# Whole blocks stored stripe by stripe, and the column marks summed on GpSimd instead of VectorE

## The chip, the cores and the metric

The kernel runs on one core of a Trainium2 chip. The metric is the device time of one execution in microseconds. Five engines work side by side: TensorE (PE; its weight loads are shown as PEld), VectorE (DVE), ScalarE (ACT), GpSimd (POOL) and SyncE (SP, which here only issues DMAs). Each engine takes its instructions strictly in the order in which they were written.

## The reference

Four graph layers work on x (4096 nodes, 128 features) and one matrix adj (4096 x 4096, float32). Each is preceded by a normalisation and a ReLU, and its result is added to x:

```
h = max(layernorm(x), 0)
0: x += h @ Ws.T + (adj @ h) @ Wn.T + b          1: x += Chebyshev sum: adj @ h, 2 adj @ (adj @ h) - h
2: x += attention over adj.T (exp of leaky relu)  3: x += aggregate of gelu(s_i + d_j + b) * adj[i,j], gelu, layernorm
```

The matrix is sparse, and very unevenly so: entry (i, j) is present with probability about w_i w_j / 1024, w falling as the square root of the index, and the diagonal is full. All values are positive.

## The kernel before, in words

The host reorders the nodes and hands over adj and its transpose adjT. The 4096 rows are 32 blocks of 128 (NB). For the products the columns are cut into 16 stripes of 256 (RS for rows of the result, CS for columns). A stripe is multiplied with some blocks whole ("near" blocks, 112 pairs of stripe and block for the rows) and with the rest of its rows only where something stands in them: these rows are listed, gathered 128 at a time and called a chunk (68 chunks for row stripes, `rseg`, 74 for column stripes, `cseg`). Gathered chunks are stored again in DRAM tables r_tab and c_tab, so that later layers load them without gathering.

**The first stage** reads all of adj (64 tiles of 1 MB, `read_adj`, L766), once. For each block b:

- ACT turns it into an fp8 mask of 128 x 4096 (`mark`, L776), four mask buffers in all.
- DVE clears the diagonal (`scan`, L787), then makes three passes over the mask read as 1024 words of four marks: the largest word of each of the 16 column stripes goes into `col_raw[:, :, b]` (L791, one reduction), the words are joined with their own number (L796), and words without a mark are set to zero (L798). Then eight largest values are picked out of each segment of words (L805, MAX8) into `cand`; from these the positions of all entries are decoded later (`entries`).
- PE counts marks for the row stripes (L704), and `row_flags` and `pairs` (L635 to L683, small DVE operations and a few matmuls) turn this into the list of rows that each row stripe needs. There is one `words` tile.

When the last block is through L791, `all_marked` is set, and `col_flags` (L717, then `pairs`) makes the lists of the column stripes.

**Gathers.** All gathers go through GpSimd (L551): for layer 0 a chunk of adjT (`rseg`) and one of the features (`g`) for each of the 68 row chunks, for layers 1 and 2 the features alone, 74 `cseg` chunks and 74 chunks of attention features, 158 gathers of single entries (`e_val`) and 158 gathers of messages in layer 3 (`m`, `tau`, `e`): 736 in all. The `cseg` gathers need the column lists, so they can only begin when all 32 blocks are marked; `e_val` needs the decoded entries. Beside this GpSimd adds a bias to x (L987, four instructions of 1024 values per partition; L1008, eight of 512).

**Loads of near blocks and of tables** (`Layer.load`, L1092 and L1104; `Attention.batches`, L1206) are issued by SP into four `big` tiles. A near tile of up to four blocks is 128 partitions by up to four pieces of 256 floats; in adj and adjT each piece of 1 KB lies 16 KB from the next row's. The table stores are L730.

**Order.** A planner on the host simulates the engines with rough durations (a gather counts 1.27 us) and writes the instructions in the order of its simulated times; every generator above yields the engine, a duration and, by the rank with which it was started, a priority (lower goes first among those that could start at the same time). On the chip the order of each engine is then fixed, whatever the real times are.

Of the kernel before, what the change touches and what calls it, by code (L numbers as in the profile page):

```python
# [12 lines left out]
F32 = mybir.dt.float32  # L13
# [12 lines left out]
N = 4096  # L26
D = 128
P = 128
# [329 lines left out]
def on_dve(n):  # L358
    return "DVE", 0.16 + 1.05e-3 * n
# [16 lines left out]
GATHER = "POOL", 1.27  # L376


def sparse_stack(tc, x, adj, adjT, diag, w_self, w_neigh, b0, w1, b1, w2, att_src, att_dst,
                 msg_s, msg_d, msg_b, upd_h, upd_a, upd_b, ln_w, ln_b, out):  # L380


# [7 lines left out]
    with ExitStack() as ctx:  # L390
# [34 lines left out]
        u_tab = table("u_tab", N + 1, D)  # L425
        a_tab = table("a_tab", N + 1, D + 2)
        d_tab = table("d_tab", N, D)
        r_tab = [table(f"r_tab{s.index}", s.cap * P, RS) if s.cap else None for s in ROWS]
        c_tab = [table(f"c_tab{s.index}", s.cap * P, CS) if s.cap else None for s in COLS]

        def rows_in(tab):
            return tab[0:N, :].rearrange("(b p) d -> p b d", p=P)
# [280 lines left out]
        def col_flags(s):  # L713
            yield all_marked
            lane = yield lanes
            yield on_dve(NB)
            nc.vector.tensor_scalar(lane["f"], col_raw[:, s.index, :], EMPTY, None, op0=ALU.is_gt)  # L717
            yield from pairs(s, lane, fetch_col, seg_col, CS, col_list[s.index])

        row_list = [Event() for _ in ROWS]  # L720
        col_list = [Event() for _ in COLS]
        r_done = [Count(s.cap) for s in ROWS]
        c_done = [Count(s.cap) for s in COLS]
        all_marked = Event()

        def store(ready, t, slots, left, dst, done, size):

# [11 lines left out]
        def fetch_columns():  # L739
            for s in COLS:  # L740
                if s.cap:
                    yield col_list[s.index]
                for k in range(s.cap):
                    t = yield csegs
                    yield GATHER
                    gather(t, adj_segments, seg_col[:, s.chunk + k:s.chunk + k + 1])
                    here, left = Event(), Count(1)
                    here.set(plan.transfer(P * CS * 4))
                    plan.start(store(here, t, csegs, left, c_tab[s.index][k * P:(k + 1) * P, :], c_done[s.index],
                                     P * CS * 4), 6)  # L750
                    plan.start(give_back(left, csegs, t), 0)

# [17 lines left out]
        def mark():  # L770
            for b in range(NB):
# [6 lines left out]
                    plan.release(raws, raw_of[b, h])  # L778
                marked[b].set(plan.finish)

        def scan():
            for b in range(NB):
                yield marked[b]
                mask = mask_of[b]
                yield on_dve(32)
                own = mask.bitcast(I32)[:, b * P // 4:(b + 1) * P // 4]
                nc.vector.tensor_tensor(own, own, off_diag.bitcast(I32), op=ALU.bitwise_and)  # L787
                bare[b].set(plan.finish)
                plan.start(give_back(mask_left[b], masks, mask), 0)
                yield on_dve(WORDS)  # L790
                nc.vector.tensor_reduce(col_raw[:, :, b], mask.bitcast(F32).rearrange("p (s w) -> p s w", w=CS // 4),  # L791
                                        axis=AX.X, op=ALU.max)
                if b == NB - 1:
                    all_marked.set(plan.finish)
                yield on_dve(WORDS)
                nc.vector.tensor_tensor(words, mask.bitcast(I32), spread, op=ALU.bitwise_or)  # L796
                yield on_dve(WORDS + 250)
                nc.vector.scalar_tensor_tensor(words.bitcast(F32), mask.bitcast(F32), EMPTY, words.bitcast(F32),  # L798
                                               op0=ALU.is_gt, op1=ALU.mult)
                mask_left[b].set(plan.finish)  # L800
                for u in UNITS:
                    if u.block == b:
                        yield "DVE", 0.15 * len(u.segments) + (u.cuts[-1] - u.cuts[0]) / 960
                        for k, (lo, hi) in enumerate(u.segments):
                            nc.vector.max(cand_of[u.number][:, 8 * k:8 * k + 8], words.bitcast(F32)[:, lo:hi])  # L805
                        picked[u.number].set(plan.finish)

        picked = [Event() for _ in UNITS]
        valued = [Count(u.cap) for u in UNITS]
# [263 lines left out]
        class Layer:  # L1073
# [12 lines left out]
            def load(self):  # L1086
                for s in ROWS:
                    for i, blocks in enumerate(s.tiles(TOGETHER)):
                        t = yield bigs
                        yield SP  # L1090
                        n = len(blocks)
                        nc.sync.dma_start(  # L1092
                            as_rows(t)[:, :n, :], adjT[blocks[0] * P:(blocks[-1] + 1) * P, s.lo:s.lo + RS].rearrange(
                                "(b p) i -> p b i", p=P))
                        self.at["near", s.index, i] = t
                        self.near_here[s.index][i].set(plan.transfer(n * P * RS * 4))
                    if self.number == 0 or not s.cap:
                        continue
                    yield r_done[s.index]
                    for i, chunks in enumerate(s.groups(TOGETHER)):  # L1100
                        t = yield bigs
                        yield SP
                        n = len(chunks)
                        nc.sync.dma_start(  # L1104
                            as_rows(t)[:, :n, :], r_tab[s.index][chunks[0] * P:(chunks[-1] + 1) * P, :].rearrange(
                                "(c p) i -> p c i", p=P))
                        self.at["list", s.index, i] = t
                        self.list_here[s.index][i].set(plan.transfer(n * P * RS * 4))

            def gather(self):  # L1110
                for s in ROWS:
                    if s.cap:
                        yield row_list[s.index]
                    for c in range(s.cap):
                        if self.number == 0:
                            t = yield rsegs
                            yield GATHER
                            gather(t, adjT_segments, seg_row[:, s.chunk + c:s.chunk + c + 1])
                            here, left = Event(), Count(2)
                            here.set(plan.transfer(P * RS * 4))  # L1120
                            self.at["seg", s.index, c] = t, here, left
                            plan.start(store(here, t, rsegs, left, r_tab[s.index][c * P:(c + 1) * P, :],
                                             r_done[s.index], P * RS * 4), 2)
                            plan.start(give_back(left, rsegs, t), 0)
                        g = yield rows_g
                        yield self.table_done
                        yield GATHER
                        gather(g[:, :D], self.table, fetch_row[:, s.chunk + c:s.chunk + c + 1])
                        self.at["row", s.index, c] = g
                        self.rows_here[s.index][c].set(plan.transfer(P * D * 4))  # L1130
# [51 lines left out]
        class Attention:  # L1182
# [11 lines left out]
            def batches(self):  # L1194
                for number, (s, blocks, chunks) in enumerate(self.units()):
                    t = yield bigs
                    here = Event()
                    if chunks:
                        yield c_done[s.index]
                    n = len(blocks or chunks)  # L1200
                    yield SP
                    if blocks:
                        src = adj[blocks[0] * P:(blocks[-1] + 1) * P, s.lo:s.lo + CS]
                    else:
                        src = c_tab[s.index][chunks[0] * P:(chunks[-1] + 1) * P, :]
                    nc.sync.dma_start(t[:, :n, :], src.rearrange("(k p) i -> p k i", p=P))  # L1206
                    here.set(plan.transfer(n * P * CS * 4))
                    rows = []
                    for c in chunks or ():
                        g = yield rows_g  # L1210
                        rows.append((g, Event()))
                    if chunks:
                        plan.start(self.rows(s, chunks, rows), 0)
                    plan.start(self.attend(s, t, here, blocks, chunks, rows), number * 1e-3)
# [352 lines left out]
        with tc.tile_pool(name="scan", bufs=1) as scanning:  # L1567
# [1 line left out]
            masks = tiles(scanning, "mask", 4, (P, N), F8)  # L1569
            raws = tiles(scanning, "raw", 1, (P, HALF))  # L1570
            raws = Slots([dst[:, :HALF], dst[:, HALF:]] + raws.items)
            words = scanning.tile([P, WORDS], I32, name="words", tag="words")
            plan.filler = fill
            plan.start(read_x(), -9)
            plan.start(read_adj(), -8)
# [96 lines left out]
def gnn_stack_kernel(tc, **args):  # L1672


    some_bad = sparse_stack(tc, **args)
    with tc.If(some_bad > 0):
        args.pop("diag")
        dense_stack(tc, **args)


# [293 lines left out]
            nc.sync.dma_start(out_rows[:, s, :], o)  # L1974


# [31 lines left out]
```

## Time and profile before

| What | Value |
|---|---|
| timed runs, median of 3 | 1175.17 us (1168.04 to 1184.51) |
| profiled execution, first to last instruction | 1172.0 us |
| PE busy | 965.2 us (82%) |
| DVE busy | 887.9 us (76%) |
| POOL busy | 771.8 us (66%), 831 instructions |
| ACT busy | 577.5 us (49%) |
| DMA | 236.04 MB, mean 201 GB/s |

No separate time of the profiled execution is on hand; its span lies inside the range of the timed runs, 3.2 us under their median. "Busy" is the time in instructions; the profile puts register, semaphore and DMA-issuing instructions outside it, so an engine with a fixed pause between its instructions can be fully used at less than 100%. PE's share holds 732 filler matmuls (L617) that the planner puts into its gaps, and is no measure of a bound.

### The profile page before, as it was taken

How to read it: one execution, taken by the hardware profiler on the slowest of the kernel's cores; microseconds unless marked ns; L12 is line 12 of the kernel's file. 1: busy time of each engine (PE TensorE's matmuls, PEld its weight loads, DVE VectorE, ACT ScalarE, POOL GpSimd, SP SyncE). 2: the span in 40 equal slices, each digit the busy share in tenths (PEclk: the TensorE clock that was granted, in tenths of full speed). 3: DMA queues.
4: the chain of work that ended last, by engine and by line, in shares of the span. 5: the costliest groups of instructions: out<-in, count | busy, mean ns of one | idle time of the engine just before them, and what ended most of it. 6: DMA issues, size and time to landing. Idle time of an engine off the chain costs nothing. (4 is left out here: it accounts for less than half of the span.)

```text
span 1172.0 us, 19272 instructions
## 1 busy us (share of the span) xinstructions
PE 965.2 (82%) x5782; PEld 669.7 (57%) x5782; DVE 887.9 (76%) x3443; ACT 577.5 (49%) x1228; POOL 771.8 (66%) x831
## 2 busy tenths in 40 slices
PE   5888887878888888788888879899999976678783
PEld 2555665545555665576676654455555555566562
DVE  5799988877878886576888866665666585577895
ACT  3985556654622212232434457576767652234553
POOL 5127746545437677777777778777777777777770
PEclk9979989888789999998989989898999878889997
DMA  7999999999846978889865653443445222222321
GB/s 221 348 349 394 349 407 359 352 309 334 294 127 174 301 217 275 245 272 315 247 204 175 184 150 97 127 129 102 131 131 154 71 69 67 54 68 68 77 74 33
DMA packets 175417, 236.04 MB, mean 201 GB/s; under 512 B 22452, under 2 KB 155336, under 8 KB 167112
## 3 DMA queue, kind: packets, MB, share of 16 engines
q1 hardware_dynamic: 148904, 186.45, 46.9%
q0 software_dynamic: 26400, 48.27, 16.7%
q8 instruction: 48, 0.79, 0.3%
q14 instruction: 65, 0.53, 0.1%
HBM read 203.41 MB, written 31.23 MB: 200 GB/s over the span
## 5 line engine op out<-in xcount | busy, mean ns | idle before, releaser
L551 POOL DMA_INDIRECT e_val<-in_adj,e_at x158 | 163.0, 1032 | 48.0 <-issue 40.1
L551 POOL DMA_INDIRECT g<-h_tab,fetch_row x136 | 134.6, 990 | 41.1 <-issue 27.9
L551 POOL DMA_INDIRECT rseg<-in_adjT,seg_row x68 | 68.8, 1012 | 90.3 <-issue 42.3
L1146 PE MATMUL acc<-big,hA 128*128 128x256 f32 x448 | 122.0, 415 | 2.0 <-DMA big<-in_adjT 2.0
L617 PEld LDWEIGHTS <-nothing 128*128 128x128 f16 x732 | 74.9, 105 | 82.0 <-issue 20.7
L617 PE MATMUL pick<-nothing 128*128 128x512 f16 x430 | 114.2, 413 | 0.0
L551 POOL DMA_INDIRECT cseg<-in_adj,seg_col x74 | 70.9, 958 | 43.6 <-issue 17.3
L1146 PEld LDWEIGHTS acc<-big,hA 128*128 128x128 f32 x448 | 89.4, 210 | 14.5 <-DMA big<-in_adjT 2.6
L776 ACT ACTIVATE mask<-dst 128x2048 fp8e4<-128x2048 f32 x43 | 81.8, 1904 | 26.8 <-DMA dst<-in_adj 26.7
L551 POOL DMA_INDIRECT m<-d_tab,e_col x79 | 76.8, 972 | 24.1 <-issue 13.4
L551 POOL DMA_INDIRECT g<-a_tab,fetch_col x74 | 75.7, 1023 | 22.5 <-issue 12.5
L1163 PE MATMUL acc<-big,g 128*128 128x256 f32 x272 | 77.4, 417 | 9.7 <-DMA big<-r_tab 6.5
L1243 DVE TENSOR_TENSOR tau<-e,big 128x512 f32<-128x512 f32 (+3 forms) x61 | 54.5, 893 | 38.2 <-ACT e L1239 34.0
L551 POOL DMA_INDIRECT tau<-d_tab,e_col x67 | 66.2, 988 | 21.2 <-issue 11.3
L617 PE MATMUL bank<-nothing 128*128 128x512 f16 x302 | 79.8, 401 | 0.0
L551 POOL DMA_INDIRECT g<-u_tab,fetch_row x68 | 64.5, 949 | 20.7 <-issue 8.8
L577 ACT ACTIVATE junk<-xN,stat 128x128 f32<-128x128 f32 x128 | 51.3, 401 | 49.0 <-DVE stat L573 38.5
L1146 PE MATMUL acc<-big,hB 128*128 128x256 f32 x224 | 60.9, 411 | 11.3 <-DMA big<-in_adjT 11.3
L1163 PE MATMUL acc<-rseg,g 128*128 128x256 f32 x136 | 53.4, 501 | 16.8 <-DMA g<-h_tab,fetch_row 16.7
L898 DVE SCALAR_TENSOR_TENSOR ehit<-ehit,pos,pick 128x32 f32<-128x32 f32 (+7 forms) x158 | 38.7, 285 | 36.2 <-ACT ehit L895 35.9
L1163 PEld LDWEIGHTS acc<-big,g 128*128 128x128 f32 x272 | 52.6, 207 | 21.4 <-issue 7.5
L895 ACT COPY ehit<-pick 128x192 f32<-128x192 f32 (+7 forms) x74 | 20.4, 287 | 89.3 <-PE pick L892 78.1
(322 smaller groups left out, 2553.1 us busy)
## 6 DMA issues: line engine op xcount, KB each, us to landing
dst<-in_adj SPq DMA_DIRECT2D x43, 1024.0 KB
big<-in_adjT SPq DMA_DIRECT2D x45, 512.0 KB
raw<-in_adj SPq DMA_DIRECT2D x21, 1024.0 KB
big<-in_adjT SPq DMA_DIRECT2D x66, 256.0 KB
big<-r_tab SPq DMA_DIRECT2D x30, 512.0 KB
c_tab<-cseg SPq DMA_DIRECT2D x74, 128.0 KB
r_tab<-rseg SPq DMA_DIRECT2D x68, 128.0 KB
big<-c_tab SPq DMA_DIRECT2D x15, 512.0 KB
```

Source lines behind the costliest of these rows:

```text
L551: nc.gpsimd.indirect_dma_start(out=dst, out_offset=None, in_=table[:, :], in_offset=bass.IndirectOffsetOnAxis(ap=index, axis=0))
L577: nc.scalar.activation(junk, src[:, k, :], AF.Square, bias=st[:, 0, k:k + 1], accum_out=st[:, 1, k:k + 1])
L617: nc.tensor.matmul(idle[2][idle[1]], nothing[:, :P], nothing, start=True, stop=True)
L776: nc.scalar.activation(mask[:, h * HALF:(h + 1) * HALF], raw_of[b, h], AF.Sigmoid, scale=1e38, accum_out=marks[:, 2 * b + h:2 * b + h + 1] ...
L895: nc.scalar.copy(hit, pv[:, :, :W])
L898: nc.vector.scalar_tensor_tensor(hit[:, q, :], hit[:, q, :], pos0[:, k + q:k + q + 1], pv[:, q, W:2 * W], op0=ALU.is_le, op1=ALU.mult, acc ...
L1146: nc.tensor.matmul(acc, self.near[:, b, :D], as_rows(t)[:, k, :], start=count == 0, stop=count == every - 1)
L1163: nc.tensor.matmul(acc, row[:, :D], r, start=count == 0, stop=count == every - 1)
L1243: nc.vector.tensor_mul(tau[:, :n, :], e[:, :n, :], a[:, :n, :])
```

## The change

Two things are changed.

The layout: the host passes two further copies of the matrix, `adj_near` and `adjT_near`, in which each stripe's blocks lie one beside the other for each of the 128 partitions, and r_tab and c_tab are laid out in the same way. A near tile or a table tile of four blocks is then one run of 4 KB per partition instead of four runs of 1 KB. Numbers and sizes of the DMAs stay. The gathers still read adj and adjT.

The marks: the reduction L791 leaves DVE. In its place a new task adds up, on GpSimd, the words that L798 leaves (zero where nothing stands, positive otherwise) for each stripe: six additions that halve 64 words to 32, 16, 8, 4, 2 and 1. So `words` has two tiles, given back when both GpSimd and MAX8 are through with them, and `all_marked` counts the sums of all 32 blocks.

```diff
+        def marks_of_columns(b, words, left):
+            sums = words.bitcast(F32).rearrange("p (s w) -> p s w", w=CS // 4)
+            n = CS // 8
+            yield "POOL", 3.1
+            while n:
+                into = halved[:, :, :n] if n > 1 else col_raw[:, :, b:b + 1]
+                nc.gpsimd.tensor_add(into, sums[:, :, :n], sums[:, :, n:2 * n])
+                sums, n = halved, n // 2
+            left.set(plan.finish)
+            all_marked.set(plan.finish)
...
-                yield on_dve(WORDS)
-                nc.vector.tensor_reduce(col_raw[:, :, b], mask.bitcast(F32).rearrange("p (s w) -> p s w", w=CS // 4),
-                                        axis=AX.X, op=ALU.max)
-                if b == NB - 1:
-                    all_marked.set(plan.finish)
+                words = yield words_of
                 yield on_dve(WORDS)
                 nc.vector.tensor_tensor(words, mask.bitcast(I32), spread, op=ALU.bitwise_or)
...
                 mask_left[b].set(plan.finish)
+                left = Count(2)
+                plan.start(marks_of_columns(b, words, left), -4)
+                plan.start(give_back(left, words_of, words), 0)
...
-            words = scanning.tile([P, WORDS], I32, name="words", tag="words")
+            words_of = tiles(scanning, "words", 2, (P, WORDS), I32)
+            halved = scanning.tile([P, len(COLS), CS // 8], F32, name="halved", tag="halved")
...
-                            as_rows(t)[:, :n, :], adjT[blocks[0] * P:(blocks[-1] + 1) * P, s.lo:s.lo + RS].rearrange(
-                                "(b p) i -> p b i", p=P))
+                            as_rows(t)[:, :n, :], adjT_near[s.index * P:(s.index + 1) * P, blocks[0] * RS:(
+                                blocks[-1] + 1) * RS].rearrange("p (b i) -> p b i", i=RS))
...
-        r_tab = [table(f"r_tab{s.index}", s.cap * P, RS) if s.cap else None for s in ROWS]
+        r_tab = [table(f"r_tab{s.index}", P, s.cap * RS) if s.cap else None for s in ROWS]
...
+def by_stripe(a, size):
+    return a.reshape(NB, P, N // size, size).transpose(2, 1, 0, 3).reshape(N // size * P, NB * size)
```

The loads of r_tab, c_tab and adj_near and the stores into the tables are changed in the same way, and `col_flags` compares `col_raw` with 0.0 instead of the word of four empty marks.

More of the change, by code (lines that the diff above doesn't have):

```diff
@@ L376, with sparse_stack @@
 GATHER = "POOL", 1.27
-def sparse_stack(tc, x, adj, adjT, diag, w_self, w_neigh, b0, w1, b1, w2, att_src, att_dst,
+def sparse_stack(tc, x, adj, adjT, adj_near, adjT_near, diag, w_self, w_neigh, b0, w1, b1, w2, att_src, att_dst,
                  msg_s, msg_d, msg_b, upd_h, upd_a, upd_b, ln_w, ln_b, out):
@@ L427, in sparse_stack @@
         d_tab = table("d_tab", N, D)
-        r_tab = [table(f"r_tab{s.index}", s.cap * P, RS) if s.cap else None for s in ROWS]
-        c_tab = [table(f"c_tab{s.index}", s.cap * P, CS) if s.cap else None for s in COLS]
+        r_tab = [table(f"r_tab{s.index}", P, s.cap * RS) if s.cap else None for s in ROWS]
+        c_tab = [table(f"c_tab{s.index}", P, s.cap * CS) if s.cap else None for s in COLS]
         def rows_in(tab):
@@ L716, in col_flags @@
             yield on_dve(NB)
-            nc.vector.tensor_scalar(lane["f"], col_raw[:, s.index, :], EMPTY, None, op0=ALU.is_gt)
+            nc.vector.tensor_scalar(lane["f"], col_raw[:, s.index, :], 0.0, None, op0=ALU.is_gt)
             yield from pairs(s, lane, fetch_col, seg_col, CS, col_list[s.index])
@@ L723, in sparse_stack @@
         c_done = [Count(s.cap) for s in COLS]
-        all_marked = Event()
+        all_marked = Count(NB)
         def store(ready, t, slots, left, dst, done, size):
@@ L748, in fetch_columns @@
                     here.set(plan.transfer(P * CS * 4))
-                    plan.start(store(here, t, csegs, left, c_tab[s.index][k * P:(k + 1) * P, :], c_done[s.index],
+                    plan.start(store(here, t, csegs, left, c_tab[s.index][:, k * CS:(k + 1) * CS], c_done[s.index],
                                      P * CS * 4), 6)
@@ L806, in scan @@
                         picked[u.number].set(plan.finish)
+                left.set(plan.finish)
         picked = [Event() for _ in UNITS]
@@ L1104, in load @@
                         nc.sync.dma_start(
-                            as_rows(t)[:, :n, :], r_tab[s.index][chunks[0] * P:(chunks[-1] + 1) * P, :].rearrange(
-                                "(c p) i -> p c i", p=P))
+                            as_rows(t)[:, :n, :], r_tab[s.index][:, chunks[0] * RS:(
+                                chunks[-1] + 1) * RS].rearrange("p (c i) -> p c i", i=RS))
                         self.at["list", s.index, i] = t
@@ L1121, in gather @@
                             self.at["seg", s.index, c] = t, here, left
-                            plan.start(store(here, t, rsegs, left, r_tab[s.index][c * P:(c + 1) * P, :],
+                            plan.start(store(here, t, rsegs, left, r_tab[s.index][:, c * RS:(c + 1) * RS],
                                              r_done[s.index], P * RS * 4), 2)
@@ L1202, in batches @@
                     if blocks:
-                        src = adj[blocks[0] * P:(blocks[-1] + 1) * P, s.lo:s.lo + CS]
+                        src = adj_near[s.index * P:(s.index + 1) * P, blocks[0] * CS:(blocks[-1] + 1) * CS]
                     else:
-                        src = c_tab[s.index][chunks[0] * P:(chunks[-1] + 1) * P, :]
-                    nc.sync.dma_start(t[:, :n, :], src.rearrange("(k p) i -> p k i", p=P))
+                        src = c_tab[s.index][:, chunks[0] * CS:(chunks[-1] + 1) * CS]
+                    nc.sync.dma_start(t[:, :n, :], src.rearrange("p (k i) -> p k i", i=CS))
                     here.set(plan.transfer(n * P * CS * 4))
@@ L1676, in gnn_stack_kernel @@
     with tc.If(some_bad > 0):
-        args.pop("diag")
+        for name in ("diag", "adj_near", "adjT_near"):
+            args.pop(name)
         dense_stack(tc, **args)
@@ L1985 @@
     given = {
-        "x": np.asarray(x)[ORDER], "adj": adj, "adjT": adj.T, "diag": np.diagonal(adj).reshape(NB, P).T,
+        "x": np.asarray(x)[ORDER], "adj": adj, "adjT": adj.T,
+        "adj_near": by_stripe(adj, CS), "adjT_near": by_stripe(adj.T, RS), "diag": np.diagonal(adj).reshape(NB, P).T,
         "w_self": np.asarray(L0_gnn_W)[:, :D].T, "w_neigh": np.asarray(L0_gnn_W)[:, D:].T, "b0": L0_gnn_b,
```

## The prediction

> **What bounds the kernel now.** I read the busy shares in 40 slices first (a slice is 29.3 us).
>
> ```profile
> DVE  5799988877878886576888866665666585577895
> ...
> POOL 5127746545437677777777778777777777777770
> ...
> DMA  7999999999846978889865653443445222222321
> ```
>
> There are two stages. Up to slice 11 (some 320 us) DMA stands at 9 and DVE at 7 to 9, while POOL has room. From slice 12 on POOL stands at 7, one slice at 6 and one at 8, to the end. The busy time of each engine in chosen stretches says what the 7 means; the columns are the stretch, its length, then PE, PEld, DVE, ACT, POOL (each with its instructions), clock, DMA share, GB/s.
>
> ```profile
> 348.00:1141.00 793.00, 670.16 (x3606) 474.45 (x3606) 578.76 (x2439) 361.22 (x843) 601.45 (x610) 0.93 0.54 155
> ...
> 60.00:240.00 180.00, 151.82 (x1251) 104.54 (x1249) 163.71 (x494) 113.78 (x173) 101.30 (x94) 0.88 1.01 368
> 87.00:348.00 261.00, 218.18 (x1706) 146.61 (x1704) 222.88 (x702) 143.97 (x221) 139.73 (x135) 0.86 0.92 329
> ```
>
> POOL's instructions in order of time show the pause between two gathers, and the holes of the first stage:
>
> ```profile
> 290.16 1.45 POOL L551 DMA_INDIRECT g<-h_tab,fetch_row  x1 [0.30 <-issue]
> 295.01 1.27 POOL L1008 TENSOR_TENSOR xN<-xN,b_sb 128x512 f32<-128x512 f32 x1 [3.40 <-ACT hB L585]
> 302.59 1.19 POOL L551 DMA_INDIRECT rseg<-in_adjT,seg_row  x1 [6.31 <-PE acc L1163]
> 304.08 0.94 POOL L551 DMA_INDIRECT g<-h_tab,fetch_row  x1 [0.30 <-issue]
> ...
> 348.03 0.96 POOL L551 DMA_INDIRECT cseg<-in_adj,seg_col  x1 [14.61 <-DVE pf L641]
> ```
>
> Each gather is followed by 0.30 us that nothing else can use. From 348 to 1141 us POOL is busy 601.45 us in 610 instructions; with 610 x 0.30 = 183 that is 784 of 793 us, so 9 us are free. **POOL bounds everything after 348 us**, one gather per 1.25 us, and what delays it by a microsecond delays the end by one. The chain that ended last agrees: it runs from the last gathers (1140 to 1145 us) through the last normalisation. Before 348 us POOL has slack: from its first gather at 87 us it is busy 139.73 us in 135 instructions, with pauses 180 of 261 us, which leaves **81 us free**. The listed holes split them: 22 us up to 209 us, 45 from there to 332, 14 in the last wait, for the first column list. How the change spends these 81 us is the whole question.
>
> **The marks on POOL.** The rows that come nearest to the new additions, and the DVE reduction that goes:
>
> ```profile
> L791 DVE TENSOR_REDUCE col_raw<-mask 128x16 f32<-128x1024 f32 x32 | 39.1, 1221 | 2.1 <-ACT mask L776 0.4
> L1008 POOL TENSOR_TENSOR xN<-xN,b_sb 128x512 f32<-128x512 f32 x8 | 10.5, 1310 | 10.4 <-issue 6.9 <-ACT hB L585 3.4
> ```
>
> An undisturbed L1008 takes 1.27 us for 512 values per partition, an undisturbed L987 2.36 us for 1024: 0.18 us plus 2.13 ns per value. The six additions of a block take 16 x (32+16+8+4+2+1) = 1008 values, so 1008 x 2.13 ns + 6 x 0.18 = **3.23 us**. Below: the fixed part vanishes when they follow each other, 2.15 us. Above: the additions wait for DVE. L987 at 67.74 us took 3.18 instead of 2.36 us beside L798; two such waits in a block give 4.9 us. I take 3.7, the sum from the rows and half a wait, nearer to the undisturbed rows, which are most.
>
> Six blocks were reduced before 87 us, when POOL had nothing to gather; those are free. The other 26 cost 26 x 3.7 = 96 us (56 to 127). Stage by stage: up to 209 us there are 13 blocks, 48 us into 22 free, 26 left over; from 209 to 332 another 13, 48 into 45, 29 left over; the last hole takes 14 of overdue gathers of layer 0, so **15 us** run past 348. That is with every hole used. They are not all usable: POOL stands in them for buffers that PE must free (six of 6.3 us), or for ACT before L1008 (3.4 us), with the gathers queued behind, and a sum that waits for L798 now stands in the same queue. I lose a quarter of the 67 us ahead of 332, **17 us** (bounds: none, half). Sum: +32 us.
>
> **What waits for the sums.** The first column list needs the sum of block 31. L791 of that block ended at 326.7 us; L798 ends at 331.5, and with 3.7 us the mark is there at 335.2, while the list's first operation (L717) stood at 332.8: +2 us, inside the hole where overdue gathers run. With them gone it would be 2 us at the end. Behind the sum on POOL stand `rseg` and `g`, for which PE's layer 0 waits. On DVE, L796 of block b+2 waits for the sum of block b; behind it stand `pairs` and with it the next row list. At 9.4 us a block this wait costs nothing unless POOL is two blocks late.
>
> **DVE.** The reduction takes 1.14 us of DVE per block from start to start, 36 us in all. What comes in is a lock, seen in DVE's and POOL's instructions:
>
> ```profile
> 72.71 2.35 POOL L987 TENSOR_TENSOR xN<-xN,b_sb 128x1024 f32<-128x1024 f32 x1 [1.79 <-DVE pair_total L649]
> ```
> ```profile
> 72.76 2.32 DVE L651 SCALAR_TENSOR_TENSOR pst<-pst 128x1 f32<-128x1 f32 x1
> ```
>
> L651 is one value wide and otherwise takes 0.16 us; here it ends when POOL's addition ends. I summed the excess of DVE's instructions during the twelve L987 and L1008: 12.4 us in 20.7 us of additions, 60%. Where MAX8 was running (39.14 us), there was none. Sums of 3.23 us would cost DVE 1.9 us a block at 60%, and less since MAX8 (1.4 us) runs first: 0 to 1.9, I take 1.1. So DVE's saving of 1.14 is given back, net 0, between -36 and +25 us over the stage; DVE is busy 163.71 of 180 us there, so a loss would lengthen the scan. The first row list comes up to 6 us sooner by the early reductions, minus the stalls: 3 us, which the +2 above cancels.
>
> The Trainium skill's page SBUF — State Buffer, section "Who interferes with whom", says that a reduction never contends with GpSimd, while a DVE instruction with two SBUF inputs and a GpSimd one that reads SBUF exclude each other for the whole instruction. That speaks against the change: a pass that doesn't contend is replaced by six that do. The rows agree on the lock, but not on every microsecond: blocked all the time, DVE would lose 3.23 x 32 = 103 us for 36 saved, by the 60% measured at most 62.
>
> **The layout.** By 330 us 17, 22, 2 and 2 near tiles of 512, 256, 384 and 128 KB were loaded, 15.7 MB. At full DMA share the mixed 1 KB and 512 B traffic of 450 to 500 us moved 251/0.84 = 299 GB/s, and the best 10 us of the first stage, mostly 8 KB rows of adj, 413 at 1.06, so 390: 52 against 40 us, so 0 to 12 us of DMA time. I expect half of it on the DMA engines and none at the end: POOL, not DMA, then sets the first stage. After 348 us DMA is at 0.54, and the free 9 us on POOL bound the gain. The stores, the number of DMAs and SP's queue stay as they are.
>
> **Sum.** 1172.0 + 32 + 2 - 3 + 0 = 1203; the median lies 3.2 us above the profiled span, so **1206 us**.
>
> **Rivals.**
> - *The holes hide the sums* (not slower). At 3.23 us a block 20 us are left over at 209 us, 13 x 3.23 = 42 fit into 45, and the last hole takes 14 of the 17: +3, with holes fully used; at 2.15 nothing is left over, and the first list 6 us sooner gives -6. For it: the holes come twice in 18.8 us, just where two blocks are scanned. Against it: up to 163 us POOL has almost no hole. It decides below 3.3 us a block and no hole lost: 1169 to 1187.
> - *The locks feed each other.* DVE blocked by six additions, additions by L796 and L798 (1.22 us each), gathers behind both, row lists later. At 4.9 us a block: 127 + 17 - 81 = 63, and DVE's +25 in part: +55 to +85, 1230 to 1260.
> - *The scan gets faster*, over 2%: DVE gains 36 us, DMA 12. The gathers cannot: POOL's 180 us and 26 x 2.15 us end no sooner than 87 - 6 + 236 = 317, and only if the scan is also 31 us sooner is the end at 1144.
> - *Nothing changes in the packets* (runs still cut to 1 KB): worth nothing at the end here.
>
> **How the numbers follow.** The POOL overflow (+15 to +55, 1190 to 1230) has 0.56, the hidden sums 0.22, the lock loop 0.16, the fast scan 0.06. 2% is 23.5 us, about what these runs, 1.4% apart, can tell from no change: above 1198.7 lie four fifths of the overflow (0.45) and the lock loop, 0.61; faster 0.06; within, 0.33. The range, 1169 to 1250, leaves out the fast scan and the upper half of the lock loop.
>
> **What would show it.** Right: POOL at 7 or more in slices 3 to 11; about 3.7 us of additions per block; no or short holes; the first `cseg` past 355 us or layer 0's gathers past 375; then 1.25 us per gather to the end. Near packets grow and DMA's share falls. DVE's small operations of 0.16 us take 0.5 to 1.2 beside the sums. Wrong: the first `cseg` at or before 348 us with layer 0 done, additions near 2 us, or the order of gathers so altered that POOL idles after 348.

## The result, and the profile after

The changed kernel takes **1215.21 us** (median of four runs, 1213.93 to 1215.5) against 1173.94 us for the kernel before (four runs, 1168.04 to 1184.51): a ratio of **1.0326, interval 1.029 to 1.0363**, so it is slower. The profiled execution of after has a span of 1213.5 us, 41.5 us more than the 1172.0 us of before. In three of the sessions further down every kernel, the one before too, ran about 27% longer (1512.96, 1486.64 and 1485.22 us for before), at a granted clock of 0.80 to 0.84 in place of 0.90 to 0.93; they are called long sessions.

The busy shares of after in 40 slices (a slice is 30.3 us; they are counted from 0, as in the prediction):

```profile
DVE  6798867586677887674868797657667586477896
...
POOL 5568888887877677777777777777777776777770
...
DMA  7998888889875887888876563344445422222221
```

POOL stands at 7 or 8 from slice 3 to slice 12, with one 6 to come; before, it had 3 to 7 in slices 3 to 11. DMA has gone from 9 to 8 in slices 3 to 8, and DVE falls to 5 and 6 at times where it had 7 and 8. The stretches shown of before read so in after (stretch, length, then PE, PEld, DVE, ACT, POOL with their instructions, clock, DMA share, GB/s):

```profile
348.00:1141.00 793.00, 674.88 (x3580) 468.15 (x3581) 568.58 (x2430) 352.90 (x811) 597.81 (x614) 0.92 0.55 158
...
60.00:240.00 180.00, 135.60 (x1024) 89.05 (x1025) 135.62 (x399) 94.38 (x143) 143.00 (x172) 0.79 0.88 309
87.00:348.00 261.00, 201.30 (x1509) 131.19 (x1507) 191.70 (x553) 128.48 (x195) 213.57 (x258) 0.82 0.88 302
```

From 87 to 348 us POOL is busy 213.57 us where it was busy 139.73. Every other engine does less in the same time than before: DVE 191.70 for 222.88, DMA 302 GB/s for 329. The whole stage has become slower, and POOL is the one engine that does more in it. In order of time POOL now looks like this, early in the stage and at its end (start, duration, instruction, and in brackets the idle time before it):

```profile
92.98 0.95 POOL L551 DMA_INDIRECT rseg<-in_adjT,seg_row  x1 [0.31 <-issue]
93.95 1.26 POOL L788 TENSOR_TENSOR halved<-words 128x512 f32<-128x512 f32 x1
95.30 1.99 POOL L788 TENSOR_TENSOR halved<-halved 128x256 f32<-128x256 f32 x4
97.37 0.22 POOL L788 TENSOR_TENSOR col_raw<-halved 128x16 f32<-128x16 f32 x1
97.73 0.96 POOL L551 DMA_INDIRECT g<-h_tab,fetch_row  x1
...
388.73 0.95 POOL L551 DMA_INDIRECT g<-h_tab,fetch_row  x1 [0.30 <-issue]
389.98 0.95 POOL L551 DMA_INDIRECT cseg<-in_adj,seg_col  x1 [0.30 <-DVE sel L632]
```

The holes of 6.3 us and the last one of 14.61 us are gone. The last gather of layer 0 starts at 388.7 us (before 364.3), and the first `cseg` goes out at 390.0 (before 348.0), with nothing but the fixed 0.30 us ahead of it. The costs by group (count, then total busy us, mean ns, then idle time before them):

```profile
L788 POOL TENSOR_TENSOR halved<-halved 128x256 f32<-128x256 f32 (+3 forms) x128 | 67.9, 531 | 10.0
...
L788 POOL TENSOR_TENSOR halved<-words 128x512 f32<-128x512 f32 x32 | 41.7, 1303 | 34.4 <-DVE words L806 29.6 <-DVE pf L709 4.4
...
L788 POOL TENSOR_TENSOR col_raw<-halved 128x16 f32<-128x16 f32 x32 | 10.2, 320 | 2.5
```

(41.7 + 67.9 + 10.2) / 32 = 3.74 us of busy time per block.

### The profile page after: what moved, and what is told of

Read it like the earlier page. It is cut to its first block, busy times and chain, and to the rows that moved or that the text cites. A ratio compares the mean times of both kernels' runs of the same rounds, so it can differ in the third digit from the quotient of the medians.

```text
span 1213.5 us, 19481 instructions
## 1 busy us (share of the span) xinstructions
PE 984.3 (81%) x5798; PEld 673.7 (56%) x5798; DVE 884.7 (73%) x3411; ACT 576.5 (48%) x1228; POOL 893.0 (74%) x1023
## 2 busy tenths in 40 slices
DMA packets 122171, 236.05 MB, mean 195 GB/s; under 512 B 22452, under 2 KB 75592, under 8 KB 113864
## 4 chain that ended last, share of the span: by engine, by line
DVE 29%; PE 22%; DMA 21%; POOL 12%; issue 9%; ACT 4%; SPq 1%; DVEq 0%; POOLq 0%; ACTq 0%
DMA g<-h_tab,fetch_row 5%; POOL e_val L551 5%; PE acc L1158 3%; DMA g<-a_tab,fetch_col 3%; DMA m<-d_tab,e_col 2%; PE acc L1272 2%; PE acc L1274 2%; PE bank L604 2%; POOL g L551 2%; DMA cseg<-in_adj,seg_col 2%; DMA tau<-d_tab,e_col 2%; DMA raw<-in_adj 2%; POOL halved L788 2%; PE bank L617 2%; PE pick L617 2%
## 5 line engine op out<-in xcount | busy, mean ns | idle before, releaser
L617 PEld LDWEIGHTS <-nothing 128*128 128x128 f16 x748 | 79.5, 108 | 89.2 <-issue 28.7
L1158 PE MATMUL acc<-big,hA 128*128 128x256 f32 x448 | 126.1, 424 | 0.9 <-DMA big<-in_adjT_near 0.9
L617 PE MATMUL pick<-nothing 128*128 128x512 f16 x421 | 117.0, 432 | 0.0
L551 POOL DMA_INDIRECT m<-d_tab,e_col x79 | 77.8, 985 | 24.1 <-issue 13.1
L1175 PE MATMUL acc<-rseg,g 128*128 128x256 f32 x136 | 51.5, 476 | 53.5 <-DMA g<-h_tab,fetch_row 53.3
L617 PE MATMUL bank<-nothing 128*128 128x512 f16 x327 | 88.5, 409 | 0.0
L776 ACT ACTIVATE mask<-dst 128x2048 fp8e4<-128x2048 f32 x43 | 81.8, 1903 | 12.7 <-DMA dst<-in_adj 12.6
L551 POOL DMA_INDIRECT tau<-d_tab,e_col x67 | 65.4, 976 | 25.7 <-issue 13.1
L788 POOL TENSOR_TENSOR halved<-halved 128x256 f32<-128x256 f32 (+3 forms) x128 | 67.9, 531 | 10.0
L788 POOL TENSOR_TENSOR halved<-words 128x512 f32<-128x512 f32 x32 | 41.7, 1303 | 34.4 <-DVE words L806 29.6
L630 ACT ACTIVATE sel_t<-iota_row,mids 128x512 f32<-128x512 f32 (+3 forms) x43 | 27.1, 643 | 79.1 <-DVE mids L625 75.8
```

Source lines behind the costliest of these rows:

```text
L551: nc.gpsimd.indirect_dma_start(out=dst, out_offset=None, in_=table[:, :], in_offset=bass.IndirectOffsetOnAxis(ap=index, axis=0))
L617: nc.tensor.matmul(idle[2][idle[1]], nothing[:, :P], nothing, start=True, stop=True)
L630: nc.scalar.activation(lane["t"][:, :n * P], iota_row[:, :n * P], AF.Abs, bias=mids[:, g:g + 1])
L776: nc.scalar.activation(mask[:, h * HALF:(h + 1) * HALF], raw_of[b, h], AF.Sigmoid, scale=1e38, accum_out=marks[:, 2 * b + h:2 * b + h + 1] ...
L788: nc.gpsimd.tensor_add(into, sums[:, :, :n], sums[:, :, n:2 * n])
L1158: nc.tensor.matmul(acc, self.near[:, b, :D], as_rows(t)[:, k, :], start=count == 0, stop=count == every - 1)
```

## The experiments

Theory A: GpSimd's time ahead of the gathers is what costs. Theory B: the strife of GpSimd and VectorE over the words. Theory C: the planner's new order. Theory D: the layout. Theory E stands in the texts of its runs. Each ratio is to the kernel before in the same session.

In a long session GpSimd does not set the end: in the second run with memsets it is busy 463.8 us from 348 to 1141 us, in 482 instructions; with 0.30 us for each that is 608 of 793 us, and 185 are free. So the times of those runs say little of the change. Three of the kernels also have a run outside the long sessions.

### The layout alone

The marks stay on VectorE, with one tile of words:

```diff
-                words = yield words_of
+                yield on_dve(WORDS)
+                nc.vector.tensor_reduce(col_raw[:, :, b], mask.bitcast(F32).rearrange(...), axis=AX.X, op=ALU.max)
...
-                plan.start(marks_of_columns(b, words, left), -4)
```

> The layout alone; the marks stay a reduction on VectorE. Theory A (GpSimd's time): no additions on GpSimd, so its 81 us of free time before 348 us stay free and the end moves by what the scan gains: 1166 to 1176 us, the first cseg gather at 338 to 350 us. Theory B (the lock on VectorE) and theory C (the new order and the later list) expect the same. Rival D (the rows of 32 KB pitch or the two further copies slow the DMAs, whose rate fell from 344 to 302 GB/s in the changed kernel): 1185 us or more and a DMA rate of the first stage near 300 GB/s.

> The layout alone a second time, because the chips of the first calls ran every kernel, the one before too, at some 1500 us, with stage two no longer bound by GpSimd. If the kernel before is near 1174 us beside it: theories A, B and C 1166 to 1178 us and a first cseg at 338 to 352 us; rival D (the layout slows the loads) 1185 us or more. If it is near 1500 again: the same ratio as before, 0.988 to 0.998.

The first: 1509.39 us against 1512.96, ratio 0.9932 (0.988 to 0.9983). The second: **1170.09 us against 1176.44, ratio 0.9971 (0.9941 to 1.0)**. POOL's busy share in the second one's 40 slices:

```profile
POOL 5127746445446777777777777777777777777770
```

Its `cseg` gathers (count; durations in ns as min, median and max; first and last start in us):

```profile
L551 POOL DMA_INDIRECT cseg<-in_adj,seg_col x74: 942/946/1151, 338.9 to 579.1; - x74
```

POOL has its holes again (4 to 6 in slices 5 to 11), and the column lists come 9 us sooner than before. The layout doesn't cost anything; it may be worth up to 0.6%. Theory D falls: over the stretch from 87 to 348 us this kernel moves 329 GB/s, like before (after 302; the 344 in the first text is not the figure of this stretch). The loss comes in with the marks.

### Seven memsets in place of the six additions

VectorE reduces again, and the changed kernel's order, tiles and waits are kept. GpSimd is held for the same time, but touches nothing of VectorE's:

```diff
-            while n:
-                into = halved[:, :, :n] if n > 1 else col_raw[:, :, b:b + 1]
-                nc.gpsimd.tensor_add(into, sums[:, :, :n], sums[:, :, n:2 * n])
-                sums, n = halved, n // 2
+            for _ in range(7):
+                nc.gpsimd.memset(idle, 0.0)
...
+                nc.vector.tensor_reduce(col_raw[:, :, b], mask.bitcast(F32).rearrange(...), axis=AX.X, op=ALU.max)
                 words = yield words_of
```

> As the run without additions, but GpSimd writes seven times 512 zeros per partition for each block (0.48 to 0.54 us each in the profile of before, some 3.5 us a block): its time is taken, and nothing is read. Theory A: the loss is there without the additions' two inputs, 1200 to 1218 us, GpSimd without holes. Theory B (VectorE is held up by the additions' lock): 1168 to 1182 us.

> The new layout, the order of the changed kernel and its waits are kept; the column marks are taken by VectorE's reduction again, and in place of each block's six additions GpSimd runs seven memsets of 128x512, 533 ns each in the earlier run of this kernel, so 3.73 us per block against 3.74 us for the additions. The memsets read nothing that VectorE writes. Theory A (what costs is GpSimd's time in front of the gathers, 26 blocks x 3.7 us): 1195 to 1220 us where the kernel before takes about 1175, first read of a column segment past 375 us. Theory B (what costs is the strife of the two engines over the words): the loss goes with the additions, 1165 to 1182 us, first read of a column segment before 355 us. If the kernel before takes about 1490 us on this chip, A is seen in the first read alone and the time stays within 2%.

> The seven memsets per block once more (VectorE's reduction for the marks, the changed kernel's order and waits, 7 x 533 ns = 3.73 us of GpSimd per block that touch nothing of VectorE's). Where the kernel before takes about 1175 us on this chip: theory A (GpSimd's time in front of the gathers) says 1195 to 1220 us and a first read of a column segment past 370 us; theory B (the strife over the words) says 1165 to 1182 us and a first read before 355 us. Where the kernel before takes about 1490 us: within 2% by both.

In the long sessions: 1470.37 us, 0.9802 (0.9709 to 0.9896), and 1468.85 us, 0.9937 (0.9888 to 0.9986). In the third: **1203.45 us against 1173.1, ratio 1.0268 (1.0223 to 1.0312)**. POOL's slices in its profile:

```profile
POOL 6558888888887677777777777877777776777770
```

The group of its memsets, and then its `cseg` gathers:

```profile
L785 POOL MEMSET idle<- 128x512 f32 x224 | 119.5, 534 | 11.2
```
```profile
L551 POOL DMA_INDIRECT cseg<-in_adj,seg_col x74: 942/946/1192, 380.9 to 620.6; - x74
```

POOL is as full as in after. 119.5 / 32 = 3.73 us per block, with nothing to quarrel over, give 30.35 of the 41.27 us. Theory A is shown for the greater part. The other 10.9 us are open: the strife may have a part in them, but the two intervals just overlap, and this kernel also keeps the reduction on VectorE. As it has the changed order too, theory C is not told apart from A by this run alone; but with the memsets POOL is idle beyond its short pauses for only 8.8 us up to 440 us (below), so something else can hardly have been what it waited for.

### The sums for a part of the blocks

From block 6 or 19 on VectorE reduces, and GpSimd has nothing to add:

```diff
+                if b >= ON_POOL:
+                    yield on_dve(WORDS)
+                    nc.vector.tensor_reduce(col_raw[:, :, b], mask.bitcast(F32).rearrange(...), axis=AX.X, op=ALU.max)
+                    all_marked.set(plan.finish)
                 words = yield words_of
...
-                left = Count(2)
-                plan.start(marks_of_columns(b, words, left), -4)
+                left = Count(1 + (b < ON_POOL))
+                if b < ON_POOL:
+                    plan.start(marks_of_columns(b, words, left), -4)
```

> New layout; only the first 6 blocks are summed on GpSimd, before it has anything to gather, the other 26 reduced on VectorE. Theory A: the sums cost nothing, the first row list comes up to 6 us sooner: 1162 to 1174 us. Theory B: 6/32 of the loss, some +8 against the layout alone. Theory C: like A.

> New layout; the first 19 of the 32 blocks summed on GpSimd, the other 13 reduced on VectorE. Theory A: 13 blocks x 3.7 = 48 us of sums after the first gather against 81 us free, so most of it is hidden: 1170 to 1188 us, and GpSimd has holes again after 209 us. Theory B: in proportion, 19/32 of 41 us: about 1198 us. Theory C (the list waits for the last sum): as with no sums, 1175 us, since the last marks are VectorE's.

> The changed kernel with GpSimd's sums for blocks 0 to 18 alone, and VectorE's reduction for 19 to 31. GpSimd is given 13 blocks x 3.74 = 49 us after its first gather, in place of 97. Theory A (GpSimd's time, with the holes of this stage used whole): 49 us fit into the 81 us that were free, so most is hidden, 1168 to 1188 us. Theory E (every microsecond put in front of the gathers costs the same share, 41.5/97): 13/26 of the loss, 1188 to 1200 us. If the kernel before takes about 1490 us on this chip, neither is told by the time.

> GpSimd's sums for blocks 0 to 18 alone once more, VectorE's reduction for 19 to 31: 13 blocks x 3.74 = 49 us of GpSimd after its first gather in place of 97. Where the kernel before takes about 1175 us on this chip: theory A (the 81 us in which GpSimd had nothing to do in this stage take the sums up first, and only what is over delays the gathers) says 1168 to 1188 us, first read of a column segment by 362 us; theory E (every microsecond put in front of the gathers delays them by the same share, 41.5 of 97) says 1188 to 1200 us, first read at 366 us or later. Where the kernel before takes about 1490 us: within 2% by both.

Long sessions: six blocks 1510.93 us, 0.9977 (0.9948 to 1.0007); nineteen 1494.88, 0.9912 (0.9864 to 0.996), and 1477.37, 0.9934 (0.9888 to 0.9981). Nineteen blocks in the third: **1192.45 us against 1175.4, ratio 1.0123 (1.0085 to 1.0161)**. That is under 2%, with an interval clear of 1, and the time lies in theory E's range, not A's. It also goes against theory C as this kernel's first text has it: the list can't have waited for the last sum, which ended at 235 us. The first read of a column segment, at 363.0 us, lies between the two (by 362, or 366 and later). POOL's slices:

```profile
POOL 5568888864546677777777777877777776777770
```

POOL in order of time after its last sum, which ended at 235 us, and then the `cseg` gathers:

```profile
301.17 0.94 POOL L551 DMA_INDIRECT g<-h_tab,fetch_row  x1 [0.30 <-issue]
307.61 0.94 POOL L551 DMA_INDIRECT rseg<-in_adjT,seg_row  x1 [5.50 <-issue]
...
331.47 0.94 POOL L551 DMA_INDIRECT g<-h_tab,fetch_row  x1 [0.30 <-issue]
339.89 0.94 POOL L551 DMA_INDIRECT rseg<-in_adjT,seg_row  x1 [7.49 <-PE pick L617]
```
```profile
L551 POOL DMA_INDIRECT cseg<-in_adj,seg_col x74: 940/946/1172, 363.0 to 603.8; - x74
```

The holes are back in slices 8 to 12 (4 to 6), and yet the column lists are 15 us late. Free time late in the stage did not make up for what was lost early: what is late by then is the scan. This is followed below.

### The marks alone, the additions left away, the additions twice

The marks alone: before's layout with after's marks. Without additions: the memset kernel above with no memset. Twice: the six additions are run once into `halved` alone and then again:

```diff
+            for into_marks in (False, True):
+                part, n = sums, CS // 8
+                while n:
+                    into = halved[:, :, :n] if n > 1 or not into_marks else col_raw[:, :, b:b + 1]
+                    nc.gpsimd.tensor_add(into, part[:, :, :n], part[:, :, n:2 * n])
+                    part, n = halved, n // 2
```

> The marks alone on GpSimd, the blocks laid out as before. Theories A, B and C: all of the loss, 1208 to 1225 us, first cseg near 390 us, GpSimd without holes from 88 us on, DMA rate near 300 GB/s although the rows are 1 KB again. Rival D: 1175 to 1190 us.

> The changed kernel in its own order of instructions, the planner still counting 3.1 us of GpSimd for each block, but no addition is issued; the reduction stands on VectorE again, at a place that the planner gives no time. Theory A: GpSimd is free again: 1165 to 1182 us, first cseg 335 to 355 us. Theory C (the order that the planner made): it keeps most of the loss, 1200 us or more.

> The changed kernel, its order kept, with the six additions of each block made twice (the first time into a scratch tile). Theory A: GpSimd has no hole left after 88 us, so another 26 x 3.3 to 3.9 us go straight into the time: 1300 to 1320 us. Theory B: VectorE loses another 1 to 1.9 us a block: 1245 to 1275 us. Theory C: no change, 1215 us.

All three fell in long sessions. The marks alone: 1494.17 us, 0.9889 (0.9849 to 0.9928); without additions: 1485.82, 0.9974 (0.9924 to 1.0024); twice: **1579.13, 1.0622 (1.0527 to 1.0717)**. The first `cseg` of the marks alone, then of twice:

```profile
L551 POOL DMA_INDIRECT cseg<-in_adj,seg_col x74: 940/946/1144, 395.2 to 712.1; - x74
```
```profile
L551 POOL DMA_INDIRECT cseg<-in_adj,seg_col x74: 940/946/1155, 502.5 to 815.0; - x74
```

A second set of sums moves the first read by 107 us, about the 27 x 3.74 = 101 us that such a set takes after the first gather (the two kernels differ in layout and session too). So even where the end has another bound, the first stage follows GpSimd's time once it is full. In the other kernels of these sessions the first read came between 381 and 403 us, with sums and without (384.3 for the layout alone, 338.9 in the session where the kernel before took 1176), so their ratios below 1 say nothing for the change where the kernel before takes 1174.

Theory C can be set against these traces. In after, with the memsets, without additions and with the additions twice, the work of GpSimd, VectorE and ScalarE and the DMAs of SyncE come in one and the same order, marks left aside. Yet the first read is at 390.0 us in after and at 502.5 in twice, though twice fell in a long session; with the memsets it comes at 381 us in long and other sessions alike. And in one session, at the same order, SP waits between 60 and 390 us for late chunks (L730) 7.2 us without additions and 83.8 us with the memsets. So GpSimd's time, and not the order alone, moves the first stage. That the order costs nothing is not shown: the kernel without additions has the latest of those other first reads, 403.0 us, although its chunks were not late, and it was run in a long session only.

## Why the prediction was right

The forecast was 1206 us, slower, range 1169 to 1250; 1215.21 was measured. POOL's time from its first gather up to 440 us, when all five kernels were long gathering without holes, shows the balance. All values are in us and summed from the trace's instructions; of each idle time the first 0.31 us count as pause, the rest as hole.

| Kernel | Length | Gathers: number, busy | Sums or memsets | Bias | Pauses | Holes |
|---|---|---|---|---|---|---|
| before | 352.8 | 197, 196.0 | 0 | 10.5 | 60.3 | 85.9 |
| layout alone | 355.2 | 203, 202.2 | 0 | 10.5 | 61.9 | 80.5 |
| 19 blocks | 359.8 | 185, 188.0 | 53.7 | 10.2 | 61.4 | 46.6 |
| memsets | 360.9 | 178, 180.8 | 101.0 | 10.4 | 59.9 | 8.8 |
| after | 358.6 | 171, 172.8 | 102.7 | 10.2 | 60.2 | 12.7 |

**The cost per block** was right: 3.74 us for a predicted 3.7, and made up as it was worked out. 18 of the 32 blocks took 3.23 to 3.31 us, the 3.23 of the sum from the rows; single additions that took up to 1.0 us longer make the rest, and the longest block took 5.23. 27 blocks, not 26, fell behind the first gather, which came at 81.4 us for 87.2 (up to 6 us sooner had been named). What the sum did not have is the idle time between the additions of a block, 0.08 us each, 10.6 us in all after the first gather; the prediction had only asked whether a fixed part vanishes there. It also gave every gather a pause of 0.30 us, which the traces show between two gathers alone: in the lines of after above the first addition starts 0.02 us after a gather, and the next gather 0.14 us after the last one.

**The overflow** was right in size, in part by luck. Of the 102.7 us of sums 85.9 - 12.7 = 73.2 went into holes and 5.9 into the earlier start, and 26 gathers were displaced. 26 x 1.25 = 32.5 us; the sum had +32. But up to the first `cseg` only 7.5 us of holes were left of before's 81.4, where the prediction gave 17 up: this term was too large by more than half, and the 27th block and the idle time between the additions, which no term had, made up for it.

**After 348 us** POOL is the bound, as said, 1.25 us per gather. The last gather starts at 1183.6 us for 1144.5, 39.1 later, 6.6 more than the gathers missing at 440 us. POOL's idle time above 0.30 us from 400 to 1141 us is 12.2 us for 3.1, one hole of 5.55 us at 1008 us among it; the tail is 29.9 us for 27.5. These 9 us are the most of what lies between forecast and result, and no term had them.

**DVE's net 0** was right. DVE is busy 884.7 us for 887.9, although a pass of 39.1 us is gone: 35.9 us went into longer instructions, 1.12 us a block for the 1.1 of the prediction. The groups of the two passes over the words (count, then total busy us, mean ns, then idle before them) show that they took little of it:

```profile
L804 DVE TENSOR_TENSOR words<-mask,spread 128x1024 int32<-128x1024 int32 x32 | 42.9, 1342 | 5.2 <-ACT mask L776 2.2
L806 DVE SCALAR_TENSOR_TENSOR words<-mask,words 128x1024 f32<-128x1024 f32 x32 | 41.0, 1280 | 1.0
```

Before they took 39.5 and 39.1 us, so 5.3 us more; the rest fell on many short operations, such as 30 `hit` operations of 128x128 that took 13.1 us for 8.8. Beside the memsets, DVE is busy 899.7 us, 11.8 more than before with the same work, so some 24 us came with the additions proper. It didn't set the end: from 60 to 240 us it was busy 135.62 of 180. Against 119.8 us of additions the 35.9 us are 30%, half of the 60% taken from before's twelve bias additions, and near the 1.1 of 3.23 us (34%) that the prediction took of it. Most of this strife ended off the path, as after and the kernel with memsets are 10.9 us apart. One sign hardly came: of VectorE's operations that take under 0.2 us in before, 6 of 532 took 0.5 to 1.25 us between 30 and 390 us (before, 2 of 663). The Trainium skill's SBUF — State Buffer, section "Who interferes with whom", has the two exclude each other for whole instructions; this case's loss lies well under the 119.8 us that would follow from that rule, as an estimate, if all additions met DVE for their whole length.

**The layout** was right at "none at the end" within 0.3%, and a little low: 0.9971 (0.9941 to 1.0). In the run of the layout alone the queue of the loads takes 46.3% of 16 engines' 1165.4 us for 46.9% of 1172.0, 10 us less. That is over the whole span; the 0 to 12 given for the layout were for the near tiles up to 330 us.

**The step that failed** is "What waits for the sums": it left the scan where it was, the last mark at 335.2 us, +2. The last sum ended at 374.1 us, because the scan itself came late:

| Kernel | SP waits for late chunks | TensorE waits for late features | ScalarE waits for adj | Last load of adj issued | First cseg | Last gather | Time against before |
|---|---|---|---|---|---|---|---|
| before | 64.2 | 16.7 | 37.2 | 308.1 | 348.0 | 1144.5 | |
| layout alone | 74.0 | 18.0 | 28.5 | 304.0 | 338.9 | 1137.3 | -6.35 |
| 19 blocks | 125.8 | 37.6 | 21.7 | 330.1 | 363.0 | 1161.9 | +17.05 |
| memsets | 131.8 | 32.7 | 18.3 | 342.3 | 380.9 | 1172.0 | +30.35 |
| after | 156.8 | 53.3 | 13.2 | 349.5 | 390.0 | 1183.6 | +41.27 |

All values are in us, the waits from 60 to 390 us; ScalarE's is for both tiles into which adj is loaded (`dst` and `raw`). The loads of adj stand in SP's queue, in one fixed order with the table stores, and a store waits for its gathered chunk. Two of SP's longest waits in this stretch, first in before, then in after (line and what it waited for, us in total, times, longest):

```profile
SPq L730 <- DMA rseg<-in_adjT,seg_row: 64.2, 31, 5.0
...
SPq L766 <- ACT mask L776: 49.4, 26, 5.3
```
```profile
SPq L730 <- DMA rseg<-in_adjT,seg_row: 156.8, 48, 8.5
...
SPq L766 <- ACT mask L776: 24.4, 12, 4.9
```

The stores wait 93 us longer for late chunks, and the loads of adj behind them wait only half as long for their own buffers (24.4 for 49.4): this reads as buffers that are free and a queue that isn't. But it is not the only way from a late gather to a late scan. TensorE's products of layer 0 wait for late features, and in order with them stand the counts of the marks (L704), for which VectorE waits in turn (L709). And ScalarE waits less for adj than before, where loads that come late would make it wait more. The rows of before, then of after:

```profile
ACT mask L776 <- DMA dst<-in_adj: 23.5, 12, 3.5
...
PE acc L1163 <- DMA g<-h_tab,fetch_row: 16.7, 13, 3.4
...
DVE pf L709 <- PE bank L704: 0.4, 1, 0.4
```
```profile
ACT mask L776 <- DMA dst<-in_adj: 10.9, 6, 5.8
...
PE acc L1175 <- DMA g<-h_tab,fetch_row: 53.3, 24, 6.7
...
DVE pf L709 <- PE bank L704: 17.8, 6, 6.5
```

So late gathers hold up the engines behind them, SyncE and TensorE among them; which of these ways sets the pace of the scan is open, as no kernel with the stores on another queue, or with the counts ahead of layer 0, was tried. Either would explain why the partial kernel lost 17 us with 46.6 us of holes left, where theory A in its simple form (free time first, then the overflow) missed. The way that the prediction named, VectorE waiting for a sum before it may write the next words, did not delay the scan: in after VectorE waits for GpSimd once between 60 and 390 us, for the last sum:

```profile
DVE pf L717 <- POOL col_raw L788: 6.1, 1, 6.1
```

**The rivals.** The holes did not hide the sums: at 3.74 us it was over the 3.3 that this rival needed. The locks did not feed each other: six blocks took 4.9 to 5.3 us, the mean 3.74, and DVE had time to spare. The fast scan did not come, and packets did grow (175417 to 122171).

**Better than both** no kernel is shown to be. The layout alone is the candidate, at 0.9971 with an interval that ends at 1.0.

## What to carry to other kernels

Count an engine's fixed pauses with its busy time before calling it free: GpSimd at 54% busy had 81 us of 261 left, and 27 sums of 3.74 us used up all but 7.5. Free time counts only where it lies: what a task put in front of gathers early in a stage cost was not made good by holes later; by then the delay had passed on to other engines that work in a fixed order, and to the scan. Holding the engine with work that touches nothing, for the same time, tells its time apart from strife over memory.

## What the runs showed of the hardware that was not expected

The same kernel, the one with memsets, took 1468.85 us in one session and 1203.45 in another. Its first read of a column segment came at 381.2 and 380.9 us; the rest is later. Most instructions take as long (a gather of `g` from `h_tab` 957 and 963 ns after 390 us), TensorE's some per cent longer (L1156 with `hA`: 466 for 421 ns, with `hB` 423 for 404); what grows most is waiting. Two of the longest waits after 390 us in the long run (us in total, times, longest):

```profile
POOL g L551 <- PE acc L1173: 73.3, 23, 20.6
...
ACT hB L1059 <- remote: 49.5, 1, 49.5
```

The first is 6.0 us in the other run, and the second has no releaser that the profile of this core could name. One chip number is listed for a long session and for a short one, so the chip alone is not the cause. In the three long sessions two to four kernels ran beside the kernel before, in the others one; whether that matters was not tried. The cause stays open.
